# Order of the two products, place of VectorE's sums, and turns of the background work in an attention loop

## The chip, the cores and the metric

The kernel runs on one core of one Trainium2 chip. The metric is the device time of one execution in microseconds. Five engines work side by side, each through its own instructions in their written order: PE (matmuls, with PEld for its weight loads), DVE (VectorE), ACT (ScalarE), POOL (GpSimd) and SP, which here only issues DMAs. They meet through semaphores, and a tile's buffer can only be written again when its last reader is done.

## The reference, cut to what matters

Two layers on eight images of 128 channels by 36 x 36 pixels. Layer 0 is a group norm, convolutions, an attention over pixels and a residual. Layer 1 takes the 1296 pixels as tokens, and its attention has scores made with a tanh:

```python
q = jnp.einsum('bld,ed->ble', x, Wq) + bq
k = jnp.einsum('bld,ed->ble', x, Wk) + bk
t = jnp.tanh(q[:, :, None, :] + k[:, None, :, :])
scores = jnp.einsum('bijd,d->bij', t, w) + bw[0]
attn = jax.nn.softmax(scores, axis=-1)
```

After it comes a mixture of 64 experts, each of which picks 8 tokens of an image.

The tanh of a sum over 1296 x 1296 x 128 triples is what costs. The kernel writes it as a sum of fractions: for groups of five or six channels (16 groups of five, 8 of six) it builds, from exponentials of signed sums, matrices `qf` (per query) and `kf` (per key) such that a product over 32 or 64 rows gives a group's denominator and another its numerator. The score of a group is numerator / denominator, and the scores are added up over the groups.

## The kernel before, in words

**The loop.** The work of layer 1's scores is cut into units (image b, chunk c of 432 queries, tile j of 128 keys): 8 x 3 x 10 of them, and per chunk one unit more for the 16 keys that are left over (`rem`), sixth in order. A full unit has 12 slots (`SLOTS`, the entries k = 0 to 11), in triples: two slots of fives (two groups of 32 rows each, so they use half of the PE's rows, and the half alternates) and one slot of sixes (k = 2, 5, 8, 11; two groups of 64 rows, all of the PE's rows). A left-over unit has two slots, so there are 2928 slots. `slots` holds them all, and the loop at L1113 walks through them once, p being the slot's number.

In each slot p the loop issues

- `numerators(p)` (L977): two 432-column products into two PSUM tiles of the pool `ps_n`. That pool has four buffers, and the background's matmuls take theirs from it too (`aux`).
- `denominators(p + LAG)` (L960, LAG = 3): the two products of the slot three ahead, into one `d` tile of two banks (pool `ps_d`, two buffers), and then on ACT their logarithm, Ln (L972, 128x864); after every second slot ACT also takes the exponential of the negated pair, Exp (L975, 128x1728). The result `lq` holds the reciprocals.
- `terms(p, ns)` (L982): DVE multiplies the numerators with `lq`. In eight of twelve slots the two products go to an SBUF tile `rp` (L1003, two instructions), and POOL adds it to a running sum (L1010, L1012; `rpp` has three buffers). In the four slots of `DVE_PAIRS` DVE does the adding too (L992 to L994, L997, L999: three or four instructions on PSUM), so that these PSUM tiles are free only when the adds are done. All of it is fp32.

At a unit's end POOL folds its sum (L1019) and adds DVE's sum (L1021), and seven slots later ACT takes the exponential of the scores (`e`, L1032).

**The background.** Everything else (the next image's group norm, convolutions, layer 0's attention, its tokens and its `keys`, the weighted sums of layer 1, the gating of the experts, new `qf` blocks) is written as generators in four lanes, `first_of_all`, `urgent`, `gates` and `background`. A generator yields either before a group of matmuls or before the reading of one (`TAKE`). Once per slot `take_turns` (L1072), ahead of the slot's products, lets lanes that wait for a reading go on, and `matmul_turn` (L1077), at the slot's end, lets at most one lane issue matmuls. Both are held back by k: outside `first_of_all`, `take_turns` does nothing in a slot of `DVE_PAIRS`, and `matmul_turn` does nothing in the slot before one. `matmul_turn` also keeps a `balance` that loses the columns issued and gains `PACE` in each slot (L1087); below zero no lane but `first_of_all` may go on. The places of the background's instructions in each engine's order are thus fixed when the program is built.

In the kernel before, `DVE_PAIRS` are the slots of sixes, so the background's matmuls stand after the first five and after the six of each triple, and none after the second five.

Of the kernel before, what the change touches and what calls it, by code (L numbers as in the profile page):

```python
# [27 lines left out]
NKT = len(KT)  # L28
# [27 lines left out]
IN_TURN = [m + i for m in range(NF // 2) for i in (0, NF // 2)]  # L56
LAG = 3
SHIFT = 6.5
DVE_PAIRS = (2, 5, 8, 11)
PACE = 400  # L60

# [7 lines left out]
def kernel(  # L71
# [58 lines left out]
    with ExitStack() as loop, ExitStack() as score:  # L130
# [277 lines left out]
        def conv_keys(b):  # L408
            k = convolved["k"] = big_tile("k0")
            if b == 0:  # L410
                taps["k"] = load_taps("wk_t")
            for r0, nr in KROWS:
                yield from conv_turns(
                    taps["k"], (r0, nr), 1, grid(k[:, r0 * WV : (r0 + nr) * WV], WV), True
                )
# [371 lines left out]
        def gating(b):  # L787
            yield from gate_logits(b, range(NCH))
            yield from gate_tokens(b)
# [114 lines left out]
        def residuals(n):  # L904

            for b in range(n):
                res.append(big_tile("res")[:, :N])
                nc.sync.dma_start(res[b], t2d[b])
                yield step()
# [10 lines left out]
        units = [(b, c, j) for b in range(NB) for c in range(NCH) for j in order]  # L920
        slots = []
# [4 lines left out]
        def prefetch(u):  # L926
            if u < len(units) and u not in kf_of:
                b, c, j = units[u]
                assert (b, j) in made
                n = 128 if j < NKT - 1 else 32  # L930
                kf = kfp.tile([128, NF, 128], F32, tag="kf", name="kf")
                nc.sync.dma_start(
                    kf[:, :, :n], kd[b][j].rearrange("p (q t) -> p q t", t=128)[:, :, :n]
                )
                kf_of[u] = kf
# [6 lines left out]
        def products(u, k, part, outs):  # L942

            b, c, j = units[u]
            kf = kf_of[u]
            if j < NKT - 1:
                q, rows = SLOTS[k]
                for h in range(2):
                    mm(outs[h][:, :CH], kf[rows[h], q, :], qf_of[b, c, q][rows[h], part, :],  # L949
                       start=True, stop=True)  # L950
                return
            for out, bank in zip(outs, REM_SLOTS[k]):
                for i, (q, rows) in enumerate(bank):
                    mm(out[32 * i : 32 * i + 32, :CH], kf[rows, q, :32],  # L954
                       qf_of[b, c, q][rows, part, :], start=True, stop=True)

        def banks(u, k):
            return 2 if units[u][2] < NKT - 1 else len(REM_SLOTS[k])

        def denominators(p):  # L960

            if p >= len(slots):
                return
            u, k = slots[p]
            d = ps_d.tile([128, 2, 512], F32, tag="d", name="d")
            n = banks(u, k)
            products(u, k, 0, [d[:, h, :] for h in range(n)])
            if k % 2 == 0:
                lq_of[u, k // 2] = lp.tile([128, 4, CH], F32, tag="lq", name="lq")
            lq = lq_of[u, k // 2]  # L970
            o = 2 * (k % 2)
            nc.scalar.activation(lq[:, o : o + n, :], d[:, :n, :CH], AF.Ln)  # L972
            if k % 2 == 1:
                some = lq[:, : o + n, :]
                nc.scalar.activation(some, some, AF.Exp, scale=-1.0)  # L975

        def numerators(p):  # L977
            ns = [ps_n.tile([128, 512], F32, tag="n", name="n") for _ in range(banks(*slots[p]))]
            products(*slots[p], 1, ns)
            return [ps[:, :CH] for ps in ns]  # L980

        def terms(p, ns):  # L982

            u, k = slots[p]
            lq = lq_of[u, k // 2]
            o = 2 * (k % 2)
            mult = nc.vector.tensor_mul
            rem = units[u][2] == NKT - 1
            if k in DVE_PAIRS and not rem:
                if k == DVE_PAIRS[0]:  # L990
                    live["d"] = acc.tile([128, CH], F32, tag="accd", name="accd")
                    mult(live["d"], ns[0], lq[:, o, :])  # L992
                    mult(ns[1], ns[1], lq[:, o + 1, :])
                    nc.vector.tensor_add(live["d"], ns[1], live["d"])  # L994
                else:
                    for h in range(2):
                        mult(ns[h], ns[h], lq[:, o + h, :])  # L997
                    for h in range(2):
                        nc.vector.tensor_add(live["d"], ns[h], live["d"])  # L999
            else:  # L1000
                rp = rpp.tile([128, 2, CH], F32, tag="rp", name="rp")
                for h, n in enumerate(ns):
                    mult(rp[:, h, :], n, lq[:, o + h, :])  # L1003
                if rem:
                    live.setdefault("rem", []).extend(rp[:, h, :] for h in range(len(ns)))
                elif k == 0:
                    live["r"] = rp
                elif k == 1:
                    live["p"] = acc.tile([128, 2, CH], F32, tag="accp", name="accp")
                    nc.gpsimd.tensor_add(live["p"], live["r"], rp)  # L1010
                else:
                    nc.gpsimd.tensor_add(live["p"], live["p"], rp)  # L1012
            if k % 2 == 1:
                lq_of.pop((u, k // 2))
# [11 lines left out]
        def exps(p, u, d):  # L1026
            b, c, j = units[u]

            while urgent and len(es.get((b, c), ())) == 1:
                urgent.run(p)  # L1030
            e = etp.tile([128, CH], F32, tag="e", name="e")
            nc.scalar.activation(e[:, : d.shape[-1]], d, AF.Exp, bias=eb_s)  # L1032
            es.setdefault((b, c), {})[j] = e
            if (b, c) == (NB - 1, NCH - 1) and len(es[b, c]) == NKT - 2:
                urgent.append(attend_early(b, c, es[b, c]))
            if len(es[b, c]) == NKT:
                urgent.append(attend(b, c, es.pop((b, c))))
# [30 lines left out]
        balance = [0]  # L1068

        def take_turns(p, k):  # L1072
            for lane in lanes:
                if lane.due(p, False) and (k not in DVE_PAIRS or lane is first_of_all):
                    lane.run(p)

        def matmul_turn(p, k):  # L1077


            before = behind[0]  # L1080
            for lane in lanes:
                while lane.due(p, True) and behind[0] == before:
                    paced = balance[0] < 0 or k + 1 in DVE_PAIRS
                    if lane is not first_of_all and paced or lane is gates and urgent:
                        break
                    lane.run(p)
            balance[0] = min(balance[0] - (behind[0] - before) + PACE, 2 * PACE)  # L1087

# [24 lines left out]
        for p, (u, k) in enumerate(slots):  # L1113
            b, c, j = units[u]
            rem = j == NKT - 1
            if k == 0:
                prefetch(u + 2)
                if c == 0 and j == 1:
                    if b > 0:
                        gates.append(gating(b - 1))  # L1120
                    if b == NB - 1:
                        gates.append(residuals(4))
                    if b + 1 < NB:
                        background.extend(
                            (normal(b + 1), conv_keys(b + 1), layer0(b + 1), tokens(b + 1),
                             keys(b + 1, range(NKT)))
                        )
            take_turns(p, k)
            ns = numerators(p)
            denominators(p + LAG)  # L1130
            terms(p, ns)
            if pending and pending[0][0] <= p:
                exps(p, *pending.popleft()[1:])
            last = p + 1 == len(slots) or slots[p + 1][0] != u

            if j == order[-1] and u + 1 < len(units) and k % 3:
                used = IN_TURN.index(SLOTS[k][0]) + 1
                if used < NF:
                    first_of_all.append(new_block(*units[u + 1][:2], IN_TURN[used]))
            elif j == order[-2] and last and u + 2 < len(units):  # L1140
                first_of_all.append(new_block(*units[u + 2][:2], IN_TURN[0]))
            matmul_turn(p, k)
            if last and rem:
                first_of_all.append(rem_scores(p, u, live.pop("rem")))
            elif last:
                pending.append((p + 7, u, sums(u)))
# [211 lines left out]
```

The softmax here doesn't subtract the row's maximum and nothing guards it: scores larger than these inputs give would overflow.

## Time and profile before

| | |
|---|---|
| time, median of 3 runs | 6138.14 us (6136.29 to 6141.58) |
| the profiled execution: its span, first to last instruction | 6139.0 us |
| time of the profiled execution around its span | not recorded beyond the span, which is 0.9 us over the median |
| mean granted TensorE clock | 0.985 |
| the loop over the slots, first product of DVE to its last | 162.9 to 5989.0 us: 5826 us |
| PE busy | 5957.9 us (97%), and 2862.1 us of weight loads beside it |
| ACT busy | 5279.9 us (86%) |
| DVE busy | 4796.4 us (78%) |
| POOL busy | 4597.7 us (75%) |
| DMA | 270.87 MB, mean 44 GB/s |

The span is cut by instructions: "busy" is the time in which an engine has at least one instruction under way. Matmuls on different rows of the PE overlap, and their ends are modelled, so PE's 97% does not say that it does all that it could; how close two starts follow on each other says more. In lists of groups the columns are: line, engine, operation, tiles written and read, shapes, count, then busy us and mean ns of one, then the engine's idle time before them and what ended it.

### The profile page before, as it was taken

What the parts mean: (1) busy time and instruction counts of PE and PEld (TensorE: products, weight loads), DVE (VectorE), ACT (ScalarE), POOL (GpSimd) and SP (SyncE); (2) the same over time, 40 slices, a digit from 0 to 9 for tenths busy, and PEclk for the clock granted to TensorE, in tenths of its full rate; (3) what the DMA queues carried; (4) which work ended last, traced back from release to release, by engine and by line L of the source; (5) the groups of instructions that cost most, each with busy time, mean ns of one, the idle gap of its engine ahead of it and who ended that gap; (6) DMA issues with size and microseconds to landing.
All of it is one profiled execution on the core that took longest, in us unless ns stands there. A gap on an engine that the chain in (4) does not pass through costs nothing.

```text
span 6139.0 us, 93072 instructions
## 1 busy us (share of the span) xinstructions
PE 5957.9 (97%) x33480; PEld 2862.1 (47%) x33480; DVE 4796.4 (78%) x9521; ACT 5279.9 (86%) x5371; POOL 4597.7 (75%) x2819
## 2 busy tenths in 40 slices
PE   7999999999999999999999999999999999999996
PEld 5454444544544445444455444454444544544443
DVE  4787878877788787877888777887778877788882
ACT  1888898888988888889998889888898888999990
POOL 4777777777787777778778786877777777787870
PEclk9999999999999999999999999999999999999997
DMA  1210011100110002100111001110011100110008
GB/s 44 70 37 22 25 62 38 34 25 28 68 43 20 26 27 71 39 24 23 44 55 39 22 24 59 44 39 22 20 65 40 34 25 28 58 50 29 28 20 297
DMA packets 151519, 270.87 MB, mean 44 GB/s; under 512 B 45648, under 2 KB 76752, under 8 KB 151056
## 3 DMA queue, kind: packets, MB, share of 16 engines
q1 hardware_dynamic: 151056, 264.92, 13.0%
q8 instruction: 264, 4.33, 0.3%
q14 instruction: 199, 1.63, 0.1%
HBM read 200.41 MB, written 64.19 MB: 43 GB/s over the span
## 4 chain that ended last, share of the span: by engine, by line
PE 77%; ACT 7%; DVE 6%; issue 6%; POOL 2%; DMA 1%; SPq 0%; DVEq 0%; POOLq 0%; ACTq 0%
PE n L949 37%; PE d L949 12%; PE pa L284 7%; PE pc L284 5%; ACT lq L972 5%; PE s L284 3%; PE pk L284 3%; PE pq L284 3%; DVE rp L1003 2%; DVE n L997 1%; DVE accd L999 1%; PE d L954 1%; ACT lq L975 1%; DMA w<-in_weight_dram 1%; PE n L954 1%
## 5 line engine op out<-in xcount | busy, mean ns | idle before, releaser
L1012 POOL TENSOR_TENSOR accp<-accp,rp 128x864 f32<-128x864 f32 x1440 | 2915.8, 2025 | 1041.0 <-DVE rp L1003 948.8
L949 PE MATMUL n<-qf,kf 32*128 32x432 f32 (+1 forms) x11520 | 3325.3, 574 | 46.5 <-ACT e L1032 13.3
L949 PE MATMUL d<-qf,kf 32*128 32x432 f32 (+1 forms) x11520 | 2991.6, 561 | 38.7 <-ACT lq L972 38.2
L972 ACT ACTIVATE lq<-d 128x864 f32<-128x864 f32 x2928 | 2524.2, 878 | 542.6 <-PE d L949 512.1
L1003 DVE TENSOR_TENSOR rp<-n,lq 128x432 f32<-128x432 f32 x3912 | 2173.3, 600 | 743.5 <-PE d L949 542.8
L975 ACT ACTIVATE lq<-lq 128x1728 f32<-128x1728 f32 (+1 forms) x1464 | 2398.2, 1638 | 46.3
L949 PEld LDWEIGHTS n<-qf,kf 32*128 32x128 f32 (+1 forms) x11520 | 1206.4, 184 | 1600.3 <-DVE rp L1003 581.5
L949 PEld LDWEIGHTS d<-qf,kf 32*128 32x128 f32 (+1 forms) x11520 | 1090.0, 185 | 422.1 <-issue 224.7
L997 DVE TENSOR_TENSOR n<-n,lq 128x432 f32<-128x432 f32 x1440 | 814.9, 608 | 142.1 <-PE n L949 88.5
L999 DVE TENSOR_TENSOR accd<-n,accd 128x432 f32<-128x432 f32 x1440 | 866.3, 602 | 24.6
L1010 POOL TENSOR_TENSOR accp<-rp 128x864 f32<-128x864 f32 x240 | 485.2, 2022 | 197.7 <-DVE rp L1003 195.6
L711 POOL TENSOR_SCALAR qf<-qf,cs_s 128x432 f32<-128x432 f32 x192 | 260.9, 1365 | 45.0 <-ACT qf L710 44.4
L284 PEld LDWEIGHTS pa<-xh,e 128*108 128x108 f32 x1920 | 222.5, 174 | 131.1 <-DVE rp L1003 56.0
L1021 POOL TENSOR_TENSOR accd<-accp,accd 128x432 f32<-128x432 f32 x240 | 265.2, 1105 | 18.8
L1019 POOL TENSOR_TENSOR accp<-accp 128x432 f32<-128x432 f32 x240 | 264.4, 1102 | 16.7
L284 PE MATMUL pa<-xh,e 128*108 128x129 f32 x1920 | 262.9, 283 | 8.7 <-ACT e L1032 5.2
L284 PE MATMUL s<-q,k 128*116 128x432 f32 x480 | 230.3, 568 | 1.7 <-DVE q L316 1.4
L284 PEld LDWEIGHTS pk<-xT,a_k 128*128 128x128 f32 x1408 | 171.2, 192 | 107.0 <-DVE n L997 33.7
L462 POOL TENSOR_TENSOR tot<-tot,e 116x432 f32<-116x432 f32 x192 | 212.0, 1104 | 6.0 <-ACT e L471 4.6
L471 ACT ACTIVATE e<-s 116x432 f32<-116x432 f32 x240 | 124.9, 520 | 98.3 <-PE s L284 97.9
L284 PE MATMUL pa<-e,vw 116*128 116x432 f32 x480 | 204.6, 549 | 0.0
L284 PE MATMUL pk<-xT,a_k 128*128 128x128 f32 (+1 forms) x1408 | 202.5, 287 | 0.1
(213 smaller groups left out, 3788.4 us busy)
## 6 DMA issues: line engine op xcount, KB each, us to landing
kf<-kd SPq DMA_DIRECT2D x239, 512.0 KB
kd<-ks SPq DMA_DIRECT2D x158, 256.0 KB
w<-in_weight_dram SPq DMA_DIRECT2D x32, 1024.0 KB
wk_t<-wk_t_d SPq DMA_DIRECT2D x7, 768.0 KB
wv_t<-wv_t_d SPq DMA_DIRECT2D x7, 768.0 KB
wq_t<-wq_t_d SPq DMA_DIRECT2D x7, 768.0 KB
x<-in_x_dram SPq DMA_DIRECT2D x8, 648.0 KB
t<-tokd SPq DMA_DIRECT2D x96, 54.0 KB
```

Source lines behind the costliest of these rows:

```text
L284: mm(out, lhsT, rhs, **kw)
L711: nc.gpsimd.tensor_scalar(qf[:, 1, :], qf[:, 0, :], cs_s[:, q : q + 1], None, ALU.mult)
L949: mm(outs[h][:, :CH], kf[rows[h], q, :], qf_of[b, c, q][rows[h], part, :], start=True, stop=True)
L972: nc.scalar.activation(lq[:, o : o + n, :], d[:, :n, :CH], AF.Ln)
L975: nc.scalar.activation(some, some, AF.Exp, scale=-1.0)
L997: mult(ns[h], ns[h], lq[:, o + h, :])
L999: nc.vector.tensor_add(live["d"], ns[h], live["d"])
L1003: mult(rp[:, h, :], n, lq[:, o + h, :])
L1010: nc.gpsimd.tensor_add(live["p"], live["r"], rp)
L1012: nc.gpsimd.tensor_add(live["p"], live["p"], rp)
L1019: nc.gpsimd.tensor_add(s[:, 0, :], s[:, 0, :], s[:, 1, :])
L1021: nc.gpsimd.tensor_add(d, s[:, 0, :], d)
```

## The change

Four things, in one function's body and three conditions:

- In a slot, `denominators(p + LAG)` is issued ahead of `numerators(p)`.
- `DVE_PAIRS` becomes the second fives (1, 4, 7, 10). DVE's own sums are made there; the products of the sixes go to `rp` and POOL. The first add of POOL in a unit is then at k = 2 instead of k = 1, its last at k = 11 instead of k = 10.
- `take_turns` is held back in the second fives. `matmul_turn` is held back by the new tuple `ALONE`, the first fives, so the background's matmuls stand after the second five and after the six: on both sides of the six. In a left-over unit's slots (`in_rem`) neither is held back by k; before, the second of them was, for matmuls.
- `PACE` goes from 400 to 440.

```diff
-DVE_PAIRS = (2, 5, 8, 11)
-PACE = 400
+DVE_PAIRS = (1, 4, 7, 10)
+ALONE = (0, 3, 6, 9)
+PACE = 440
...
-                elif k == 1:
+                elif k == 2:
                     live["p"] = acc.tile([128, 2, CH], F32, tag="accp", name="accp")
                     nc.gpsimd.tensor_add(live["p"], live["r"], rp)
...
         def take_turns(p, k):
+            k = -1 if in_rem(p) else k
             for lane in lanes:
                 if lane.due(p, False) and (k not in DVE_PAIRS or lane is first_of_all):
                     lane.run(p)
 
+        def in_rem(p):
+            return p < len(slots) and units[slots[p][0]][2] == NKT - 1
+
         def matmul_turn(p, k):
-
+            k = -1 if in_rem(p) else k
 
             before = behind[0]
             for lane in lanes:
                 while lane.due(p, True) and behind[0] == before:
-                    paced = balance[0] < 0 or k + 1 in DVE_PAIRS
+                    paced = balance[0] < 0 or k in ALONE
...
             take_turns(p, k)
+            denominators(p + LAG)
             ns = numerators(p)
-            denominators(p + LAG)
             terms(p, ns)
```

## The prediction

> **What bounds the kernel now.** I read the page's totals first, then the waits, then two stretches by their windows, then single slots in the timeline. The totals:
>
> ```profile
> span 6139.0 us, 93072 instructions
> PE 5957.9 (97%) x33480; PEld 2862.1 (47%) x33480; DVE 4796.4 (78%) x9521; ACT 5279.9 (86%) x5371; POOL 4597.7 (75%) x2819
> ...
> L972 ACT ACTIVATE lq<-d 128x864 f32<-128x864 f32 x2928 | 2524.2, 878 | 542.6 <-PE d L949 512.1
> ```
>
> Two engines are near their ends: PE by its 97%, and ACT, whose idle time stands nearly all before the logarithms and is ended by the denominators' matmuls: 512.1 us. The waits, with the engine and line that waits, the one waited for, total us, times, longest:
>
> ```profile
> POOL accp L1012 <- DVE rp L1003: 948.8, 648, 6.9
> PEld n L949 <- DVE rp L1003: 581.5, 1032, 1.5
> ...
> ACT lq L972 <- PE d L949: 512.1, 665, 3.3
> ...
> PEld n L949 <- DVE accd L999: 198.5, 472, 1.6
> ```
>
> The numerators' weight loads wait for DVE to free a PSUM tile (581.5 and 198.5 us; matmuls still under way cover part of that). The denominators stand behind them in PE's order. Next a stretch with key matmuls in the background, and one with none (columns: length, then busy us of PE, PEld, DVE, ACT, POOL, clock, DMA):
>
> ```profile
> 5260.00:5286.00 26.00, 26.00 (x169) 14.53 (x162) 17.30 (x32) 24.82 (x29) 17.10 (x10) 1.00 0.30 106
> 5476.00:5494.00 18.00, 17.70 (x93) 7.60 (x90) 16.05 (x31) 17.81 (x19) 16.30 (x9) 1.00 0.09 32
> ```
>
> Without background ACT is full (17.81 of 18.00) and sets the pace. With it, neither PE's order nor ACT (24.82 of 26.00) is left waiting for one thing alone. One slot shows how they hold each other up:
>
> ```profile
> 3009.99 1.31 PE L949 MATMUL n<-qf,kf 32*128 32x432 f32 x3
> 3010.02 1.24 DVE L999 TENSOR_TENSOR accd<-n,accd 128x432 f32<-128x432 f32 x2
> ...
> 3010.67 0.18 PEld L949 LDWEIGHTS n<-qf,kf 32*128 32x128 f32 x1 [0.39 <-DVE accd L999]
> ...
> 3010.68 0.63 PE L949 MATMUL d<-qf,kf 32*128 32x432 f32 x2
> ```
>
> The second numerator waits for DVE's first add of the six before; the denominators, which need nothing of DVE, start 0.69 us after the slot did. And a six where nothing waits:
>
> ```profile
> 2019.49 1.00 PE L949 MATMUL n<-qf,kf 64*128 64x432 f32 x4
> 2020.32 0.89 PE L949 MATMUL d<-qf,kf 64*128 64x432 f32 x4
> ```
>
> Even there d stands 0.83 us behind n. In a five the two run side by side (other rows), 0.93 us for both.
>
> **How much there is to win.** For each of the 264 units I added up PE's work and ACT's, from the program's order: a five 0.93, a six 1.65 (0.83 + 0.82), a background matmul of 432 columns 0.92, of 216 0.43, of up to 129 0.27; a logarithm 0.84, a pair's exponential 1.55, the scores' exponential 0.55, other ACT steps 0.41 to 0.50, all as distances between starts in the trace. PE gets 5275 us, ACT 5123, and the larger of the two per unit, summed, 5449. The loop takes 5826. So 377 us is lost inside units because the two do not wait for each other at the right time.
>
> **The change part by part.** No instruction is added or removed: the built program has the same matmuls, and 1489 background groups before and after. SP's DMAs are the same and their issue moves by a few slots at most; the loads of `kf` still run two units ahead: 0.
>
> *A, denominators first.* In a slot d gains what n costs ahead of it: 0.83 us in each of 720 sixes, nothing in a five, and in both whatever n waits for DVE. Going through the 512 us wait by wait in the trace (with the left-over units some 540): sixes have 141 us, of which 135 lie after the moment when d could have started (its `d` buffer free, PE free); fives have 388, of which 119. With the left-overs 266 us in all. That is the upper end. The lower end is a loss: n is now behind d, which waits for ACT in 199 weight-load waits (146.1 us, "PEld d L949 <- ACT lq L972"), and if DVE's start is late by that and all of it reaches the end, 146 us are lost. Of the 266, some 105 lie in units where ACT has more work than PE; only there does time given to ACT come back whole. Elsewhere PE is as full and gets back a little by running d beside a held n. I take 110, near the 105.
>
> *B, DVE's sums in the second fives.* Four DVE instructions take 2.36 us (1.12 + 1.24 in the timeline), two take 1.12. I laid one triple out by hand, with two 0.92 us background groups, PE 5.35 us without waits. `ps_n` goes round twice per triple (eight tiles). Before, the next first five needs the six's first tile, freed by the third of the four instructions: 0.29 us late. After, the six's second tile needs the second five's first one, with a background group and d in between: 0.19 us late. So 0.10 in some 540 triples with two groups, 54 us, half of which I count in A already: 27, taken as 25. Bounds: the gain is at most the 198.5 us of waits for L999; if instead every triple got a new 0.19 us wait, 720 x 0.19 = 137 us are lost. POOL gets the same eight tiles, one slot later at the unit's end: its last add, fold and sum are 2.02 + 1.10 + 1.11 = 4.2 us after the last `rp`, and seven slots (at least 11.6 us at 19.9 us a unit) hide that: 0. If POOL were 7 us behind, `e` would hold ACT in every unit. The first `rp` is held one slot longer; with three buffers and 1041 us of POOL idle before L1012, 0.
>
> *C, where the background goes.* In the new order triples with three groups fall from 64 to 1, and a chunk's last unit loses some 3 us of PE work (24.3 to 21.9 in its first chunk), which goes to its neighbours. By the same prices the sum of the larger engine per unit becomes 5492: +43. Over groups of three slots it is 5753 to 5761 (+8), of six 5515 to 5569 (+54): bounds 8 and 54, I take 43, as units are how far work is shifted. The raised `PACE` is in these counts.
>
> A rule to weigh here: a triple with two groups changes between 32, 64 and 128 rows five times before, four times after (the step from a five to a six goes). The row for that step shows n of the six starting 0.47 us after the five's last pass (2019.02 to 2019.49), as far apart as two passes of a five (2008.62 to 2009.09), so by the row its going saves 0. The Trainium skill, "TensorEngine Tiling (Array Packing)", Key Properties, says that a change of tiling mode drains TensorE, which would make the same step worth something in each of those triples; it gives no price, and the trace shows none for this step, so the sum stays as it is.
>
> Sum: 6139.0 - 110 - 25 + 43 = 6047 us for an execution like the profiled one, whose span is 0.9 us over the median: 6046 by the median's measure. I say 6047.
>
> **Rivals.**
>
> 1. *PE is full anyway.* ACT gets its input earlier and idles later; A and B are worth nothing, C stays: 6139 + 43 = 6182, or with C at 8, 6147. For it: PE's 97%, and PE's work above ACT's in most units. Against it: 5449 of 5826, and the stretch at 5260, where 1.2 of 26 us is ACT's idle although the PE work is less than the stretch.
> 2. *Bunched denominators (the other side).* d's ends are now 0.93, 1.74 and 2.67 us apart where they were 1.85, 1.65, 1.85: n of the six, a background group and the next five's d follow each other without one for ACT. ACT has two tiles in hand, two logarithms or 1.65 us, plus an exponential (1.55) in one triple of two. Where none falls there, it waits 2.67 - 1.65 = 1.0 us. If that happens in half of some 540 triples and half of it reaches the end, 0.5 x 270 = 135 us come on top: 6047 + 135 = 6182; with A's 110 lost as well 6292. It decides once the new wait is over 92 / 270 = 0.34 us on average. Against it: the wait only counts where ACT has no slack; in my hand-laid triple PE (5.35) is above ACT (4.8).
> 3. *It unlocks more.* All of A's 266, half of B's 198.5, C at 8: 6139 - 266 - 99 + 8 = 5782; half of that way from my forecast, 5915, is as far as I believe. PE's 5275 us of work, some 550 below the loop, allows it.
>
> **How the numbers follow.** Forecast 0.48, for itself 5990 to 6110; rival 1 0.17; rival 2 0.21; rival 3 0.14. Up to 0.2% (12 us) a measurement of this kernel can't tell from none. Faster: 0.48 and 0.14, less 0.02 for forecasts that just fall short, 0.60. Same: those 0.02 and the lower edge of rival 1, 0.07. Slower: the rest, 0.33. The range takes rival 1 and the nearer half of rival 2 and part of rival 3: 5940 to 6210.
>
> **What would show it.** A: "ACT lq <- PE d" falls from 512 to under 400 us, and in sixes d starts first. B: DVE's waits before L999's successors move from the first fives to the sixes, and the n waits for accd shrink below 198 us. C: the units after a chunk's start are longer, the chunk's last one shorter. Rival 1: the ACT wait falls and the span doesn't. Rival 2: ACT's wait for d grows, at the first fives. I am wrong if PE's n waits for ACT (63.7 us now) grow by 100 us or more: then DVE is held up by the new order.

## The result, and the profile after

The changed kernel takes 6188.59 us (median of 4 runs, 6187.01 to 6189.16) against 6139.86 us before (4 runs, 6136.29 to 6142.17). The ratio is 1.0081, 95% interval [1.0067, 1.0095]: 49 us slower, where 6047 had been forecast. The profiled execution took 6187.01 us, its span is 6185.4 us. By the starts and ends of DVE's products and sums the loop went from 5826.1 to 5873.1 us, so 47 of the 49 us lie in it.

The page of the changed kernel, its totals, the shares of the chain that ended last by engine, and the logarithms:

```profile
span 6185.4 us, 92990 instructions
PE 5739.0 (93%) x33480; PEld 2861.9 (46%) x33480; DVE 4798.9 (78%) x9521; ACT 5268.5 (85%) x5371; POOL 4597.2 (74%) x2819
...
PE 55%; ACT 20%; issue 15%; DVE 8%; POOL 1%; DMA 1%; DVEq 0%; ACTq 0%; SPq 0%; POOLq 0%
...
L973 ACT ACTIVATE lq<-d 128x864 f32<-128x864 f32 x2928 | 2497.0, 879 | 540.7 <-PE n L950 400.4
```

PE is busy for 219 us less in a longer run, and the idle time before the logarithms, 542.6 us before, is 540.7. That wait is what the change was expected to cut. The waits of the changed kernel (engine and line that waits, the one waited for, total us, times, longest; lines have moved by one):

```profile
DVE rp L1004 <- PE n L950: 866.6, 1091, 12.3
PEld d L950 <- ACT lq L973: 614.4, 808, 4.6
...
ACT lq L973 <- PE n L950: 400.4, 439, 2.7
...
PE d L950 <- ACT lq L973: 171.3, 238, 3.9
ACT e L472 <- PE s L285: 124.1, 83, 67.0
...
ACT lq L973 <- PE d L950: 115.3, 154, 2.5
...
PEld n L950 <- DVE rp L1004: 86.9, 299, 1.5
...
PEld n L950 <- DVE accd L1000: 44.9, 156, 0.9
```

Before, three of these waits and DVE's products for POOL, and then the same products after:

```profile
DVE rp L1003 <- PE d L949: 542.8, 771, 12.5
PEld d L949 <- ACT lq L972: 146.1, 199, 5.0
DVE rp L1003 <- PE n L949: 51.5, 135, 2.9
...
L1003 DVE TENSOR_TENSOR rp<-n,lq 128x432 f32<-128x432 f32 x3912 | 2173.3, 600 | 743.5 <-PE d L949 542.8
```

```profile
L1004 DVE TENSOR_TENSOR rp<-n,lq 128x432 f32<-128x432 f32 x3912 | 2183.9, 601 | 950.6 <-PE n L950 866.6
```

Three things are to be seen. The numerators' loads hardly wait for DVE any more (581.5 and 198.5 us before, 86.9 and 44.9 after). In exchange the denominators' loads wait for ACT (146.1 before, 614.4 after), and DVE waits more before these products: 950.6 us, 743.5 before. (The wait that carries the name of the numerators grew from 51.5 to 866.6, but 542.8 us of before carried the name of d, which these products do not read; most of that growth is a change of label.) And ACT waits as long as ever. Most of that wait now carries the name of the numerators, but this is a question of labels: over all slots with such a wait the logarithm starts a median 47 ns after the last pass of its own d (10th to 90th percentile 46 to 47 ns), and d and n of a five end nearly together.

Where ACT waits has changed, though. I sorted its idle time before the logarithms by the kind of slot whose d it waited for (us):

| | first fives | second fives | sixes | left-over units | all |
|---|---|---|---|---|---|
| before | 166 | 223 | 142 | 12 | 543 |
| after | 420 | 39 | 67 | 14 | 541 |

The first fives took over all that the others lost. One triple of the changed kernel in the timeline (start, us, engine, line, tiles, shape, count, idle before):

```profile
2599.53 0.53 PE L950 MATMUL d<-qf,kf 32*128 32x432 f32 x2
2599.55 0.87 PE L950 MATMUL n<-qf,kf 32*128 32x432 f32 x3
...
2600.11 0.89 ACT L973 ACTIVATE lq<-d 128x864 f32<-128x864 f32 x1 [1.87 <-PE n L950]
...
2602.09 0.99 PE L950 MATMUL d<-qf,kf 64*128 64x432 f32 x4
...
2602.92 1.01 PE L950 MATMUL n<-qf,kf 64*128 64x432 f32 x4
...
2603.13 1.65 ACT L973 ACTIVATE lq<-d 128x864 f32<-128x864 f32 x2
...
2603.86 1.27 PE L285 MATMUL pc<-xwin,wv_t 128*128 128x198 f32 x6
...
2605.06 0.19 PEld L950 LDWEIGHTS d<-qf,kf 32*128 32x128 f32 x2 [0.23 <-ACT lq L973]
2605.07 0.63 PE L950 MATMUL d<-qf,kf 32*128 32x432 f32 x2
...
2606.36 1.65 ACT L973 ACTIVATE lq<-d 128x864 f32<-128x864 f32 x2
...
2608.09 1.00 PE L950 MATMUL d<-qf,kf 64*128 64x432 f32 x4
```

The six's n and a background group stand between the six's d (2602.09) and the next first five's (2605.07); then the second five follows directly. ACT gets its tiles in bunches and takes two logarithms in a row ("x2", 1.65 us). At 2600.11 it had been idle for 1.87 us, and the logarithm starts 0.05 us after the d passes begun at 2599.53 end (2599.53 + 0.53 = 2600.06), whatever the label says. Over the whole loop the ends of d are on average 0.97 us apart after a first five, 2.34 after a second five and 2.70 after a six; before it was 1.91, 2.08 and 1.98.

The 47 us show on ACT. It is busy for 11.4 us less (5279.9, now 5268.5) and the span is 46.4 longer, so its idle time has grown by 58 us. These groups of ACT hold it (busy us and mean ns, then idle time before and what ended it):

```profile
L472 ACT ACTIVATE e<-s 116x432 f32<-116x432 f32 x240 | 125.3, 522 | 124.5 <-PE s L285 124.1
L711 ACT ACTIVATE qf<-pq,fb_s 128x432 f32<-128x432 f32 x192 | 117.2, 610 | 16.9 <-PE pq L285 16.6
L688 ACT ACTIVATE ks<-pk 128x512 f32<-128x512 f32 (+1 forms) x174 | 95.8, 552 | 20.3 <-PE pk L285 19.1 <-PE n L950 1.2
```

Before, the same three were 98.3, 0.3 and 1.2 us: together +62. The scores of layer 0, the new `qf` blocks and the keys are background work whose matmuls ACT now has to wait for. It fits that the loss is made only where there is background work: the first image of the loop takes 3 us more, the next six 5 to 13 us more each, and the last, which has little of it, 9 us less (659.3, now 650.0). The two stretches shown of before have these counterparts, with columns length, busy us of PE, PEld, DVE, ACT, POOL, clock and DMA, the second with almost no background work:

```profile
5306.00:5332.00 26.00, 24.63 (x163) 14.46 (x162) 17.37 (x32) 24.20 (x28) 16.36 (x9) 1.00 0.28 102
...
5526.00:5544.00 18.00, 13.59 (x88) 5.05 (x82) 16.05 (x30) 17.84 (x18) 15.28 (x8) 1.00 0.21 84
```

In the second ACT is full as before (17.84 of 18.00). In the first neither engine is: PE 24.63 and ACT 24.20 of 26.00, where PE was at 26.00 and ACT at 24.82.

### The profile page after: what moved, and what is told of

It is laid out like the page before. It is cut to its first block, busy times and chain, and to the rows that moved or that the text cites. A ratio compares the mean times of both kernels' runs of the same rounds, so it can differ in the third digit from the quotient of the medians.

```text
span 6185.4 us, 92990 instructions
## 1 busy us (share of the span) xinstructions
PE 5739.0 (93%) x33480; PEld 2861.9 (46%) x33480; DVE 4798.9 (78%) x9521; ACT 5268.5 (85%) x5371; POOL 4597.2 (74%) x2819
## 4 chain that ended last, share of the span: by engine, by line
PE 55%; ACT 20%; issue 15%; DVE 8%; POOL 1%; DMA 1%; DVEq 0%; ACTq 0%; SPq 0%; POOLq 0%
PE d L950 19%; ACT lq L973 14%; PE n L950 13%; PE pa L285 7%; PE pc L285 5%; DVE rp L1004 4%; PE s L285 2%; ACT e L1033 2%; PE pk L285 2%; ACT qf L711 1%; ACT lq L976 1%; PE n L955 1%; PE d L955 1%; DMA w<-in_weight_dram 1%; PE pq L285 1%
## 5 line engine op out<-in xcount | busy, mean ns | idle before, releaser
L950 PE MATMUL n<-qf,kf 32*128 32x432 f32 (+1 forms) x11520 | 3009.9, 554 | 57.8 <-ACT e L472 22.3
L973 ACT ACTIVATE lq<-d 128x864 f32<-128x864 f32 x2928 | 2497.0, 879 | 540.7 <-PE n L950 400.4
L1004 DVE TENSOR_TENSOR rp<-n,lq 128x432 f32<-128x432 f32 x3912 | 2183.9, 601 | 950.6 <-PE n L950 866.6
L950 PE MATMUL d<-qf,kf 32*128 32x432 f32 (+1 forms) x11520 | 2735.6, 562 | 174.9 <-ACT lq L973 171.3
L976 ACT ACTIVATE lq<-lq 128x1728 f32<-128x1728 f32 (+1 forms) x1464 | 2398.4, 1638 | 46.4
L950 PEld LDWEIGHTS n<-qf,kf 32*128 32x128 f32 (+1 forms) x11520 | 1286.4, 185 | 766.1 <-issue 333.9
L950 PEld LDWEIGHTS d<-qf,kf 32*128 32x128 f32 (+1 forms) x11520 | 981.3, 185 | 1142.6 <-ACT lq L973 614.4
L1000 DVE TENSOR_TENSOR accd<-n,accd 128x432 f32<-128x432 f32 x1440 | 868.4, 603 | 24.7
L285 PE MATMUL pq<-xT,a_q 128*128 128x432 f32 x384 | 190.0, 577 | 31.3 <-ACT qf L711 28.7
```

Source lines behind the costliest of these rows:

```text
L285: mm(out, lhsT, rhs, **kw)
```

## The experiments

Kernels are compared with the kernel before on the same chip. Where a number of us is given for a difference, it is the difference of two medians; the kernel before has medians of 6137.58 to 6142.56 us in these comparisons. A difference between two changed kernels can join two chips, and then some 5 us of it can be the chips'.

### One part at a time

Only the denominators moved ahead, nothing else of the change:

```diff
             take_turns(p, k)
+            denominators(p + LAG)
             ns = numerators(p)
-            denominators(p + LAG)
             terms(p, ns)
```

> The kernel before with denominators(p + LAG) ahead of numerators(p) and nothing else. Theory 1 (the place of the background's turns bunches the denominators; the order of the two products by itself helps, as step A had it): 6030 to 6110 us, ACT's idle before the logarithms below 480 us. Theory 2 (denominators first is what harms, since n then stands behind d's wait for ACT and DVE is late): 6180 to 6240 us, PE's weight loads of d waiting for ACT 400 us or more (146 before, 614 after). Theory 3 (the larger PACE and the shifted background are the cause): 6030 to 6140 us.

6288.05 us, ratio 1.0237 [1.0222, 1.0253]: 146 us slower than before (6142.56), where part A had been priced at 110 us faster, and above the ranges of all three theories. The waits of this kernel:

```profile
ACT lq L972 <- PE n L949: 510.8, 650, 2.4
PEld d L949 <- ACT lq L972: 463.8, 658, 4.9
PEld n L949 <- DVE accd L999: 248.0, 478, 1.6
...
ACT lq L972 <- PE d L949: 107.8, 164, 2.5
```

ACT waits 100 us longer before its logarithms than before the change (643 against 543), and the numerators wait longer for DVE's sums (248.0 against 198.5).

The whole change without this part:

```diff
             take_turns(p, k)
-            denominators(p + LAG)
             ns = numerators(p)
+            denominators(p + LAG)
             terms(p, ns)
```

> The changed kernel with numerators first again; sums, turns and PACE as changed. Theory 1: the denominators stay bunched (0.93, 2.57, 1.85 us apart by hand) and step A's gain is gone: 6190 to 6280 us. Theory 2: the harm is gone: 6080 to 6140 us. Theory 3: 6180 to 6230 us.

6345.76 us, 1.0331 [1.0316, 1.0347], again above all three ranges. So the other parts alone cost 203 us, and denominators first, costing 146 us alone, wins 157 us among them. The parts don't add up: 146 + 203 would be 349, and the two together cost 49.

The whole change with DVE's sums left in the sixes, the background's turns as in the change:

```diff
-DVE_PAIRS = (1, 4, 7, 10)
+DVE_PAIRS = (2, 5, 8, 11)
+HELD = (1, 4, 7, 10)
...
-                elif k == 2:
+                elif k == 1:
...
-                if lane.due(p, False) and (k not in DVE_PAIRS or lane is first_of_all):
+                if lane.due(p, False) and (k not in HELD or lane is first_of_all):
```

> The changed kernel with DVE's own sums back in the sixes; readings are still held back in the second fives and matmuls in the first fives. Theory 1 and 2 alike: step B was worth 25 us, so 6190 to 6220 us. If the sums in the second fives are themselves the cause: 6110 to 6150 us.

6416.39 us, 1.045 [1.0434, 1.0465], 228 us over the changed kernel and above both ranges. Part B, priced at 25, is what makes the rest bearable.

The whole change with the background's turns as they were (`PACE` stays at 440):

```diff
+HELD = (2, 5, 8, 11)
-ALONE = (0, 3, 6, 9)
+ALONE = (1, 4, 7, 10)
...
         def take_turns(p, k):
-            k = -1 if in_rem(p) else k
             for lane in lanes:
-                if lane.due(p, False) and (k not in DVE_PAIRS or lane is first_of_all):
+                if lane.due(p, False) and (k not in HELD or lane is first_of_all):
...
         def matmul_turn(p, k):
-            k = -1 if in_rem(p) else k
```

> The changed kernel with the turns where they were (matmuls held in the second fives, readings held in the sixes, the left-over unit as before); denominators first, DVE's sums in the second fives and PACE 440 stay. Theory 1: 6050 to 6130 us, the idle of ACT before the first five's logarithm back from 420 us to under 250. Theory 2: 6170 to 6230 us. Theory 3: 6170 to 6230 us.

6176.22 us, 1.0062 [1.0045, 1.0078]: slower than before as well. This kernel is parts A and B together under the old turns, and it is 34 us over before (6142.56), where the two had been priced at 135 us faster. The changed kernel's turns then cost some 12 us more, but the two intervals overlap, and the granted clock differs: 0.982 here, 0.987 in the changed kernel. An estimate of what the clock can hold is the missing share times the span, 111 against 80 us, so at one clock the 12 could be up to 43. Its d are as uneven (1.85, 1.40 and 2.76 us apart), because now n of the six and a background group follow the six's d, and only a five's n stands between the second five's and the six's.

And `PACE` alone put back to 400 in the changed kernel:

```diff
-PACE = 440
+PACE = 400
```

> The changed kernel with PACE 400. Theory 3 (the larger PACE is the cause): 6135 to 6150 us. Theories 1 and 2: 6170 to 6210 us.

6197.0 us, 1.0094 [1.0079, 1.0109], which overlaps the changed kernel's interval. `PACE` explains nothing of the loss, as theories 1 and 2 had it.

### What DVE's own sums cost

If the adds of `DVE_PAIRS` are what turns denominators first into a loss, it should win without them. These kernels leave out DVE's adds in those slots, and with them nearly all the scores of a third of the channel groups (the first product of a unit stays); the multiplications stay, and so does everything of POOL.

```diff
                     mult(ns[1], ns[1], lq[:, o + 1, :])
-                    nc.vector.tensor_add(live["d"], ns[1], live["d"])
...
                         mult(ns[h], ns[h], lq[:, o + h, :])
-                    for h in range(2):
-                        nc.vector.tensor_add(live["d"], ns[h], live["d"])
```

The kernel before with this:

> The kernel before without DVE's adds in the sixes (L994, L999): the pair is two multiplications, 1.12 us instead of 2.36, and the sum of these slots is left out of the scores. Theory 1b: the waits of n for accd go, some 6050 to 6130 us. It is the mark for the next one.

The same with denominators first:

> Denominators first in all slots, with the same adds left out. Theory 1b (denominators first harms by the pair that loses its cover): no more than 30 us above the one without the adds and numerators first, or below it. Theory 2: 100 us or more above it, as with the adds (146).

The changed kernel with this:

> The changed kernel without DVE's adds in the second fives (the sum of these slots is left out of the scores); compare denominators first alone without the adds, 5926 us. If the changed kernel's loss is the hold by the pair: it comes down to 5926 us too, within 30. If it is the bunched denominators, which have nothing to do with the pair: 5990 to 6090 us, and ACT's idle before the first fives' logarithms stays at 350 us or more.

| | with the adds | without | ratio to before, without |
|---|---|---|---|
| before | 6139.86 | 6050.22 | 0.9859 [0.9846, 0.9873] |
| d_only | 6288.05 | 5926.50 | 0.9659 [0.9646, 0.9672] |
| after | 6188.59 | 6110.95 | 0.9949 [0.9936, 0.9963] |

Without the adds, denominators first wins 124 us (6050.22 to 5926.50); with them it costs 146. So the adds reverse the sign of part A; without them its size is near the 110 of the prediction. The waits of d_only_noadd:

```profile
PEld d L949 <- ACT lq L972: 821.8, 1027, 6.3
...
ACT lq L972 <- PE n L949: 298.0, 393, 2.1
...
ACT lq L972 <- PE d L949: 43.1, 43, 2.4
```

The denominators wait for ACT more than in any kernel shown so far (821.8 us), and n stands behind them each time, yet this is the fastest of the three. So without the adds, n behind a d that waits for ACT costs nothing that outweighs the gain. The table also shows that the adds are not the changed kernel's only trouble: without them it is slower than the old order without them, by 61 us. Its 6110.95 lies above both ranges that had been expected for it, and ACT's idle time before the first fives' logarithms is 341 us, just under the 350 named for bunching.

Part of these differences can be the granted clock, which is not the same in these three traces: 0.982 before, 0.990 in d_only_noadd, 0.977 in after_noadd. By the missing share times the span (109, 59 and 140 us) it can hold up to 50 of the 124 us and up to 31 of the 61. The signs stand without it; why the clock differs was not traced.

### Cover for the pair

The pool `ps_n` has four buffers. A pair's tiles are free only after DVE's two multiplications and two adds, so it matters what PE can do meanwhile before it comes round to the pair's first tile. From the written order, for a triple with two background groups:

| kernel | sums in | PE's work between the pair's n and the need for its first tile | n waits for L999 (L1000, L1001 where lines moved), us | time |
|---|---|---|---|---|
| before | sixes | the six's d, a group | 198.5 | 6139.86 |
| after | second fives | a group, the six's d | 44.9 | 6188.59 |
| no_turns | second fives | the six's d and n | 43.7 | 6176.22 |
| d_only | sixes | a group (d runs beside n in a five) | 248.0 | 6288.05 |
| no_d | second fives | a group (the five's d runs beside its n) | 388.5 | 6345.76 |
| no_sums | sixes | a group | 341.5 | 6416.39 |

In these six, wherever the six's d (0.83 us by itself) lies behind the pair, the kernel stays below 6190; wherever it doesn't, it takes 6288 or more. The column of waits counts numerators alone. In no_turns it is a background group that needs the pair's first tile, and the groups wait instead: their weight loads wait 420 us in all for DVE's sums, 241 before and 110 after. The largest of these waits in no_turns:

```profile
PEld pa L286 <- DVE accd L1001: 95.1, 108, 1.4
```

The next kernel was to even out the d: denominators first with the background's matmuls after both fives and none after the six, the sums still in the sixes. It takes the group away from behind the pair as well.

```diff
-                    paced = balance[0] < 0 or k + 1 in DVE_PAIRS
+                    paced = balance[0] < 0 or k in DVE_PAIRS
...
             take_turns(p, k)
+            denominators(p + LAG)
             ns = numerators(p)
-            denominators(p + LAG)
             terms(p, ns)
```

> The kernel before (PACE 400, DVE's sums in the sixes) with denominators first and the background's matmuls after both fives. The denominators come evenly, but nothing of the background stands between DVE's pair in the six and the next first five's numerators. Theory 1b: 6250 to 6400 us, no better than denominators first alone. If evenness alone decides: 6000 to 6120 us.

6876.64 us, 1.1202 [1.1185, 1.1218], far above the 6250 to 6400 that the cover alone was expected to cost. In its timeline the background's group, which needs the pair's first tile, is held by the add, and the next d behind it on PE:

```profile
2004.12 1.24 DVE L999 TENSOR_TENSOR accd<-n,accd 128x432 f32<-128x432 f32 x2
...
2004.78 0.40 PEld L288 LDWEIGHTS tpg<-ident,gt 64*108 64x108 f32 x6 [1.48 <-DVE accd L999]
2004.78 0.54 PE L288 MATMUL tpg<-ident,gt 64*108 64x64 f32 x6 [0.79 <-DVE accd L999]
...
2005.25 0.63 PE L949 MATMUL d<-qf,kf 32*128 32x432 f32 x2
```

and the numerators wait likewise:

```profile
PEld n L949 <- DVE accd L999: 527.6, 512, 1.6
```

An order with nothing but a five's d and n behind the pair is far the slowest. By my prices these are 0.93 us, as much as a background group of 432 columns, so the length of the cover alone does not rank this kernel; here it is the group that waits, and all that stands behind it on PE. The granted clock is lower too, 0.960 against 0.985 before, which by the missing share times the span can hold up to 183 of the 737 us. That the cover sets the times agrees with the six kernels of the table and with the adds' prices above (362 us in d_only, 90 before, 78 after). It is argued, not shown: the cover was not measured apart from DVE's own time for the adds, since the kernels without them relieve both, and two results below (the adds' price in fives400, and d_fives) do not follow from it.

If it were the holding of the first tile by the pair's order (multiply, multiply, add, add), freeing it after multiply, add would help. The changed kernel and the kernel before with

```diff
                         mult(ns[h], ns[h], lq[:, o + h, :])
-                    for h in range(2):
                         nc.vector.tensor_add(live["d"], ns[h], live["d"])
```

> The changed kernel with each add right behind its own multiplication (multiply, add, multiply, add), so that the first tile of the pair is free one instruction, 0.6 us, sooner. If the 0.19 us by which the six waits for the pair in my hand-laid triple costs time at the end: 6080 to 6165 us. If the bunching alone costs: 6175 to 6200 us.

> The kernel before with the same order of multiplications and adds. The 0.29 us by which the first five waits in my hand-laid triple, in some 540 triples, would be up to 150 us: 5990 to 6120 us if it reaches the end, 6125 to 6150 us if it is covered.

6177.75, 1.0057 [1.0044, 1.0069], and 6143.36, 1.0006 [0.9997, 1.0014]. About 11 us in the changed kernel, where the two intervals just overlap, and nothing before: with cover behind the pair, when exactly its first tile comes free matters little.

### Even denominators

What remains is why the changed kernel, whose pair is covered, is slower than before. Here the background's matmuls stand after both fives instead of on both sides of the six, and `take_turns` is never held; the rest of the change stays, so that a group and the six's d still lie behind the pair.

```diff
-ALONE = (0, 3, 6, 9)
+ALONE = (2, 5, 8, 11)
...
-                if lane.due(p, False) and (k not in DVE_PAIRS or lane is first_of_all):
+                if lane.due(p, False):
```

> The changed kernel with the background's matmuls after both fives and none after the six (ALONE is the sixes, readings held nowhere). Theory 1b (two things decide: what PE has to do between the slot of DVE's pair and the next numerators, and how evenly the denominators come): here a background group and the six's denominators cover the pair as in the changed kernel, and the denominators come 1.85, 1.75, 1.75 us apart by hand: 5950 to 6090 us, ACT's idle before logarithms below 400 us. If evenness is worth nothing: 6170 to 6210 us, like the changed kernel.

The same with `PACE` at 400:

> The same with PACE 400. If PACE matters by how the background is spread over the units, 6 per batch by the count of work, it is within 20 us of the one with 440.

And that one without DVE's adds, as above:

> The kernel with matmuls after both fives (PACE 400), without the adds. Bunching: well below the changed kernel without the adds, 5900 to 5960 us. Hold by the pair: within 30 us of it.

6147.17, 1.0013 [1.0004, 1.0023]; 6137.28, 0.9995 [0.9985, 1.0004]; 5963.12, 0.971 [0.9696, 0.9725]. The first falls between its two ranges: the turns are worth something, but far less than evenness had been given, and ACT's idle time before the logarithms is 519 us instead of under 400. In fives the ends of d are 1.95, 1.94 and 2.04 us apart, and ACT's idle time before the logarithms is spread (175, 189 and 122 us in first fives, second fives and sixes). Its waits:

```profile
PEld d L950 <- ACT lq L973: 711.5, 891, 4.5
ACT lq L973 <- PE n L950: 315.7, 452, 2.7
...
ACT lq L973 <- PE d L950: 161.9, 228, 1.6
```

Against the changed kernel the place of the turns is worth some 41 us with the adds (6188.59 to 6147.17, `PACE` the same in both) and 148 without them (6110.95 to 5963.12, where `PACE` differs too). Of the 148, up to 63 can be the granted clock (0.977 and 0.987). The spacing is what the two orders are made to differ in; the hold of `take_turns` differs too and was not tried by itself. So with the turns after both fives nearly all of the 49 us is gone, and fives400 is level with before. But this is a place that the kernel before did not have; against its place (no_turns) the changed turns cost some 12 us, or up to 43 at one clock.

That it is the spacing by which the turns act is not shown, and one kernel speaks against it as a rule: in d_only_noadd the ends of d are 1.69, 1.40 and 2.66 us apart, against 1.90, 1.98 and 1.89 in fives_noadd, and yet the uneven one is 37 us faster (5926.50 and 5963.12; up to 18 of them can be the clock, 0.990 against 0.987). These two differ in more than the spacing, so it is no measure of it, but evenness does not rank them. The adds' price does not follow from the cover either: it is 174 us in fives400 (6137.28 to 5963.12), where the same group and six's d lie behind the pair as in the changed kernel, in which it is 78.

### Denominators first in part, and fewer sums on DVE

Two kernels keep before's order in the sixes, where the six's d covers the pair, and put d first in all fives, or in the first fives alone:

```diff
             take_turns(p, k)
+            d_first = rem or k % 3 < 2
+            if d_first:
+                denominators(p + LAG)
             ns = numerators(p)
-            denominators(p + LAG)
+            if not d_first:
+                denominators(p + LAG)
             terms(p, ns)
```

> The kernel before with denominators first in the fives and the left-over slots only; in the sixes numerators stay first, so that DVE's pair (in the sixes) still runs under the six's denominators and a background group. Theory 1b: no cover is lost, and d no longer waits where the first five's numerators wait for the pair: 6040 to 6125 us. Theory 2 (n behind d's wait for ACT is what harms): 6160 to 6230 us, since two of three slots have it.

> The same in the first fives only, the slot whose numerators wait for the pair. Theory 1b: most of the gain of the one above, 6060 to 6130 us. Theory 2: 6145 to 6180 us.

6177.58, 1.0064 [1.005, 1.0078], and, with `d_first = k % 3 == 0`, 6184.16, 1.0073 [1.006, 1.0086]. Both are slower than before, by 40 and 47 us, where a gain had been expected from keeping the cover; d_fives lies in the range that had been given to theory 2 (n behind d's wait for ACT harms), and d_firsts just above its own. In d_fives the pair keeps its cover, and the numerators wait less for its sums than before (198.5):

```profile
PEld n L949 <- DVE accd L999: 37.8, 82, 1.2
```

So a part of what denominators first costs with the adds, some 40 us, is not the lost cover. What it is stays open. ACT's wait went from the second fives to the sixes: 177, 149 and 245 us in d_fives for first fives, second fives and sixes against 166, 223 and 142 before, and the spacing became 1.77, 2.38 and 1.84.

Two kernels give one pair fewer to DVE, so that nine slots of a unit go to POOL instead of eight. One is fives400, one the kernel before:

```diff
-DVE_PAIRS = (1, 4, 7, 10)
+DVE_PAIRS = (1, 7, 10)
```

> The kernel with matmuls after both fives (PACE 400), DVE's own sums in three slots (1, 7, 10) instead of four; the products of slot 4 go to POOL, which makes 2.02 us more in each of 240 units. The adds of four slots are worth 6137 - 5963 = 174 us there, so one slot of four some 44 us, if POOL has the room: 6060 to 6120 us. If POOL, at 4597 + 486 us, becomes the bound in the units with new query blocks: 6130 to 6250 us.

```diff
-DVE_PAIRS = (2, 5, 8, 11)
+DVE_PAIRS = (2, 8, 11)
+HELD = (2, 5, 8, 11)
```

> The kernel before with DVE's own sums in three slots (2, 8, 11), the turns held as before. The adds of four are worth 6140 - 6050 = 90 us there, one some 22 us: 6105 to 6135 us; with POOL as the bound 6140 to 6250 us.

6200.46, 1.0098 [1.0084, 1.0112], and 6156.62, 1.0025 [1.0015, 1.0036]. Both fall in the ranges given for POOL as the bound, and the traces fit that POOL has no room for it. The page of fives3, and then two of its waits:

```profile
PE 5836.3 (94%) x33480; PEld 2744.2 (44%) x33480; DVE 4566.9 (74%) x9041; ACT 5269.2 (85%) x5371; POOL 5080.7 (82%) x3059
```

```profile
DVE rp L1004 <- POOL accp L1011: 249.5, 187, 4.3
DVE rp L1004 <- POOL accp L1013: 34.3, 31, 2.2
```

In these two DVE waits 284 us for POOL to free `rp`; in the kernel before the two together are 6 us. The adds that stay on DVE cost less there than on POOL.

## Why the prediction was wrong

The sum was 6139.0 - 110 - 25 + 43 = 6047; the time is 6188.59. It went the other way, inside the range, near the 6182 at which both rival 1 and rival 2 came out (0.17 and 0.21). That it lies inside the range is luck: neither rival's sum is what the runs show.

**A, denominators first: the step that failed is "In a slot d gains what n costs ahead of it", taken as 110 us by itself.** It holds for a loop without DVE's sums (124 us). With them, moved ahead alone, it cost 146 us. It left out what the old place of the six's d was good for: standing behind the six's n it covered the pair. That the lost cover is the larger part of the 146 is the reading of the table of covers; with the cover kept (d_fives) d first in the fives still costs 40 us, which stays open. The 146 is also the lower end that I had given. That the numbers agree is chance: its reason was n standing behind a d that waits for ACT, with the loss bounded by the 146.1 us of that wait, and d_only_noadd has far more of it and is faster. With the adds that reason is not ruled out for the 40 us. Taking the gain and the loss from two different rows of the old order, when one order change makes both, was the mistake. "I take 110" should have been worked out for the whole triple in the new order, as B was.

**B, DVE's sums in the second fives: the cover was seen, the size was not.** The hand-laid triple rightly found the six's d and a group behind the pair in the new order. It compared that with the old order, where the same two stand behind it, and so found little (25). With A in the kernel the comparison is with sums in the sixes and no d behind them, and B is worth 228 us (no_sums). A and B are one step, not two terms. Together, under the old turns, they cost 34 us (no_turns) where -135 had been put down; with the turns after both fives they are worth nothing (fives400).

**C, the background's turns: the sign was right, the size is not settled, and the mechanism was another.** From before's turns to the changed ones the loss is some 12 us beside A and B (no_turns), hardly clear of noise, and up to 43 if the lower clock of no_turns is taken out; that this upper end meets the 43 of the sum is chance. Against the turns after both fives it is some 41 us (fives). I had it from PE's work shifted between units, with a chunk's last unit 2.4 us shorter and its neighbours longer. In images 1 to 6 the last unit of a chunk is shorter by 0.2, 1.1 and 0.9 us and the others move by up to 3 us either way, so that reason does not hold. What differs in fives is the place within the triple, and with it the hold of `take_turns`.

**Rival 2, bunched denominators.** Its order was right: measured 0.97, 2.34 and 2.70 us apart against 0.93, 1.74 and 2.67 laid out by hand, and the wait grew at the first fives, by 254 us. Its sum was not right: it added 135 us to a kernel that had won 110 + 25, and the second fives and sixes gave back 259 us, so that ACT's wait for d stayed at 541. Nearly all of the 49 us then appeared where no rival had looked, in ACT's waits for the background's results (+62). That these follow from the bunching is my reading: with the turns after the fives the three groups are down to 99.2, 11.0 and 14.0 us in fives, 38 us less than in the changed kernel, but why each of them waits was not traced.

**The signs.** For A, "ACT lq <- PE d" did fall below 400 us, to 115.3, and it meant nothing, since the rest had changed its label to n; the idle time before the instruction (542.6 to 540.7) was the sign to name. For B, the waits for accd fell below 198 as said (44.9), without a gain. The sign for being wrong, PE's n waiting 100 us longer for ACT, stayed silent, because the wait stands at d, one instruction ahead of n (146.1 to 614.4).

**The rule on tiling modes.** The Trainium skill, "TensorEngine Tiling (Array Packing)", Key Properties, says that a change of tiling mode drains TensorE. No run here measured such a step by itself, so it stays as in the prediction, where the row showed none of it.

Rival 1 (PE is full anyway) falls: PE's busy time fell from 97% to 93% while the kernel became slower. Rival 3 is answered by the kernels without adds: there denominators first unlocks 124 us (up to 50 of them by the clock), but not while DVE sums on these tiles.

Open stays why the even order of fives400 only reaches before's time. ACT idles 527 us there before its logarithms, as much as in the old order, and without the adds 369; whether the adds act through the four tiles or through DVE's time was not separated. How the place of the turns acts stays open as well.

## What to carry to other kernels

An instruction that stands in a queue between a product and the next use of its buffer can be cover: before moving it ahead, lay out the new order for a whole round of the buffers and price the move and the cover as one step. Where an engine in order is fed by another, count the spacing of its inputs over a round and not only how early each one is: here the wait that two kinds of slot lost came back at the third. But do not take evenness for the measure of the time, since an uneven order was the faster one in the loop without adds. Name signs by an instruction's idle time and not by the name of its releaser, which can change when two releasers end together.
